# A two-layer attention kernel: transposes of the normalized activations moved from TensorE to a DMA and ScalarE, and one product ordered in four pieces

## The chip, the cores and the metric

The kernel runs on one core of one Trainium2 chip. The metric is the device time of one execution in microseconds (us), as a median of a few runs. The profile is of one execution, taken by the hardware profiler.

## The reference, cut to what matters

The input `x` is 16 sequences of 512 tokens with 128 features, in 32-bit floats. Two layers follow, and each has an attention and a feed-forward part, both behind a normalization without weights and both added to `x`:

```python
def _layernorm(x, axis=-1, eps=1e-05):
    m = jnp.mean(x, axis=axis, keepdims=True)
    v = jnp.var(x, axis=axis, keepdims=True)
    return (x - m) / jnp.sqrt(v + eps)
...
    x = x + _L0_attn_ref(_layernorm(x, axis=-1), ...)
    x = x + _L0_ffn_ref(_layernorm(x, axis=-1), ...)
    x = x + _L1_attn_ref(_layernorm(x, axis=-1), ...)
    x = x + _L1_ffn_ref(_layernorm(x, axis=-1), ...)
```

Each attention has 16 heads of width 8 and a softmax over 512 keys. Layer 1 also normalizes queries and keys. The feed-forward part of layer 0 is a gated one (silu, hidden width 384). That of layer 1 is a linear map plus a mixture of low-rank corrections ("lora"): for each token, 8 experts are weighted by a softmax, and a product of rank 8 per expert is added.

What matters for the change: every one of the four parts needs the normalized activations transposed (features on the 128 partitions, tokens along the row), since TensorE contracts over partitions.

## The kernel before, in words

**Units.** One unit is one attention of one sequence in one layer: 16 sequences by 2 layers make 32 units. The list `units` (line 1238) starts with six units of layer 0 (`LAG`), then takes layer 1 and layer 0 in turn, and ends with six units of layer 1.

**The two big loops.** For each unit, `maxima` (line 827) computes 64 score products of 512 columns on TensorE, two at a time into a pair of PSUM banks (line 849), and VectorE takes the row maxima of each pair (line 862). The maxima are split into three 16-bit parts on GpSimd, transposed by a DMA (line 896) and written into the stacked queries, so that the second score product already has the maximum subtracted. `scores` (line 905) computes these second products (line 919), again two at a time, and ScalarE takes the exponential of each pair (line 933). `values` (line 938) multiplies the exponentials with the values and accumulates in the bank `acc` (line 950). A "step" is one such multiplication with its two pairs of exponentials: 16 steps a unit, 512 in all.

**PSUM.** Eight banks: three pairs that the maxima and the scores share, a single bank `one` that the other products use one after another (a pair stands in when `one` is taken), and `acc`.

**Around a unit.** `pre(n)` (line 695) makes the queries, keys and values of unit n: `layer_norm` (line 508), the transpose, the projections, and for queries and keys a split into 16-bit parts that six DMAs each (line 679) put into the stacks `qst` and `kst`. It begins when the scores reach step 16 (n - 3) + 3, and the maxima of unit n wait for both stacks. In layer 1 the queries and keys go through a normalization on GpSimd and six DMA transposes (line 652) first, so this chain is the longest. `post(n)` (line 993) is what follows the attention: the division, the output projection, the second normalization and the feed-forward part, `ffn0` or `ffn1`.

**The transposes.** `transposed` (line 561) makes four 128x128 transposes on TensorE into one bank (line 566), and ScalarE copies the bank to SBUF as `xT` (line 569). It is called by `pre` and, for layer 1's feed-forward part, by `post`. `halves` (line 541) serves layer 0's feed-forward part: the same four transposes (line 548), then ScalarE copies the bank twice, once rounded as `x1` (line 551) and once whole as `xT` (line 553), and GpSimd takes the difference `x2` (line 557). There are 32 calls from `pre`, 16 of `transposed` from `post` and 16 of `halves`.

**The lora product.** At the end of `ffn1` (lines 1224 to 1230) 8 small products for each sequence (four token blocks, base weights and lora weights) are issued as one block of work on TensorE.

**What sets the order.** Nothing is left to a scheduler on the chip: each engine runs its instructions in the order in which the program issues them, and a class `Plan` sets that order while the program is built. Each piece of work is a generator that yields an engine, an estimated duration, a priority and what it waits for, with a third pair of numbers for DMAs. `Plan.run` (line 181) always takes the piece that could start first by its own estimates; among those that could start within a small margin on one engine, the lowest priority number wins. On TensorE, `choose` (line 156) weighs the five kinds of work: "m" (maxima), "e" (scores), "v" (values), "x" (small products in column tiles) and "w" (full-array work such as the transposes), by constants such as `UM`, `UB`, `LATE`, `AHEAD`. `LEAD`, `LEADE` and `SHRINK` set how many steps the maxima run ahead of the scores, and how that lead shrinks near the end. `MAXPR` is the priority of the maxima's DMAs.

**Idle filler.** Before the first "v" and behind the last, TensorE is given dummy products (line 449).

Of the kernel before, what the change touches and what calls it, by code (L numbers as in the profile page):

```python
# [10 lines left out]
F32 = mybir.dt.float32  # L11
BF16 = mybir.dt.bfloat16
I32 = mybir.dt.int32
F32R = mybir.dt.float32r
AF = mybir.ActivationFunctionType
ALU = mybir.AluOpType
# [5 lines left out]
P = 128  # L22
S = 512
C = 4
# [20 lines left out]


LAG = 6
LEADE, SHRINK = 12, 2
LEAD = 19
NP = 8  # L50
VLAG = 1.59
# [5 lines left out]
HALF = 3561  # L57
GATE1 = 12000.0
EARLY = 2
MAXPR = 9.8  # L60
MAXT = 2400
DENL = 2800
PAIR = 13.08
STACK = (2600, 700)
TRANS = (3000, 500)
AHEAD = 508
DELAY = 450
UM = {"m": 1.03, "e": 1.02, "v": 0.0, "x": -0.23, "w": -0.04}
UB = {"m": 1660, "e": 1199}
LATE = 5.33  # L70
LATE_M = 2
SAME = 0
SAMEC, NEXT = 0.05, 0.0
# [18 lines left out]
def act(n, ptr=0):  # L92
    return 51 + n / 1.2 + 93 * ptr
# [218 lines left out]
def encoder_kernel(ctx: ExitStack, tc: tile.TileContext, x, wf, wi, lb, cols, rows, out):  # L312
    nc = tc.nc
# [15 lines left out]
    banks = Pairs(pairs, [single])  # L329
# [3 lines left out]
    def ring(tag, shape=None, dt=F32, bufs=2):  # L333
        if tag not in rings:
            rings[tag] = Ring(sb, shape, dt, tag, bufs)
        return rings[tag]
# [3 lines left out]
    r_xn, r_xT = ring("xn", [P, C, P]), ring("xT", [P, S])  # L340
    r_x1, r_x2 = ring("x1", [P, S], F32R, 1), ring("x2", [P, S], F32R, 1)
    r_a = [ring(f"a{k}", [P, S], BF16) for k in (1, 2, 3)]
# [8 lines left out]
    r_p = ring("p", [P, 2, S], bufs=NP)  # L351
    r_av, r_num = ring("av", [P, S]), ring("num", [P, S])
    r_y = ring("y", [P, S])
    r_den, r_rdb = ring("den", [P, 64]), ring("rdb", [P, S], bufs=1)
    r_h, r_th, r_ub = ring("h", [P, NF, S], bufs=1), ring("th", [P, S]), ring("ub", [P, S], bufs=1)
    r_lg, r_mid, r_mx = ring("lg", [P, C, E]), ring("mid", [P, C, R]), ring("mx", [P, C])
# [11 lines left out]
    w = const.tile([P, WEND], F32, name="w")  # L368
# [5 lines left out]
    ident = const.tile([P, P], F32, name="ident")  # L374
# [133 lines left out]
    def layer_norm(b_, nm, pr, waits, alone=False):  # L508
# [29 lines left out]
        r_rs.give(krs, t)  # L538
        return xn, kxn, t

    def halves(xn, kxn, t, nm, pr):

        t = yield "PE", 440, pr(), "w", (t, banks.one, r_xT, r_x1)
        b, pt = banks.take1()
        xT, kxT = r_xT.take(f"xT{nm}")
        x1, k1 = r_x1.take(f"x1{nm}")
        for c in range(C):
            nc.tensor.transpose(pt[:, c * P : (c + 1) * P], xn[:, c], ident)
        r_xn.give(kxn, t)
        tx = yield "ACT", act(S), pr(), None, (t,)  # L550
        nc.scalar.activation(x1, pt, AF.Copy)
        t = yield "ACT", act(S), pr(), None, (t,)
        nc.scalar.activation(xT, pt, AF.Copy)
        banks.give(b, t)
        t = yield "POOL", 1180, pr(), None, (t, tx, r_x2)
        x2, k2 = r_x2.take(f"x2{nm}")
        nc.gpsimd.tensor_tensor(x2, xT, x1, ALU.subtract)
        r_xT.give(kxT, t)
        return (x1, k1, tx), (x2, k2, t)

    def transposed(xn, kxn, t, nm, pr):
        t = yield "PE", 440, pr(), "w", (t, banks.one, r_xT)
        b, pt = banks.take1()
        xT, kxT = r_xT.take(f"xT{nm}")
        for c in range(C):
            nc.tensor.transpose(pt[:, c * P : (c + 1) * P], xn[:, c], ident)  # L566
        r_xn.give(kxn, t)
        t = yield "ACT", act(S), pr(), None, (t,)
        nc.scalar.activation(xT, pt, AF.Copy)
        banks.give(b, t)  # L570
        return xT, kxT, t
# [123 lines left out]
    def pre(n):  # L695
        b_, layer = units[n]
        nm = f"a_{b_}_{layer}"
        base = 16 * (n - 3) + PRE0
        pr = ramp(base, base + PRELEN, 34 if layer else 16)
# [3 lines left out]
        if layer == 0 and b_ > 0:  # L703
            t = yield "SP", 500, pr(0), None, (r_xt, gate), (2700, 700)
            load_x(b_)
            at["xt", b_, 0] = t
        xn, kxn, t = yield from layer_norm(b_, nm, pr, (("xt", b_, layer), gate), n < EARLY)
        xt = xt_of[b_]
        xT, kxT, tT = yield from transposed(xn, kxn, t, nm, pr)
        at.setdefault("go", tT)  # L710

        def residual():
# [6 lines left out]
        if layer:  # L719
            kq = None  # L720
            for g in range(2):
                t = yield "PE", 880, pr(), "x", (tT, banks.one, r_qk if g == 0 else 0.0)
                b, pt = banks.take1()
# [9 lines left out]
                t = yield "DVE", dve(S), pr(), None, (t,)  # L733
# [12 lines left out]
                t = yield "DVE", 600, pr(), None, (tg, r_ms if g == 0 else 0.0)  # L746
# [10 lines left out]
            t = yield "DVE", 400, pr(), None, (t, r_ri)  # L757
# [6 lines left out]
            t = yield "POOL", 400, pr(), None, (t, r_rt)  # L764
            nc.gpsimd.tensor_tensor(msf, msf, mhalf, ALU.mult)
            rt, krt = r_rt.take(f"rt{nm}")
            for _ in range(3):
                for k in range(4):
                    t = yield "POOL", 400, pr(0.5), None, (t - 80,)
# [11 lines left out]
            for g in range(2):  # L781
                gs = slice(8 * g, 8 * g + 8)
                t = yield "POOL", 1270, pr(), None, (t - 80,)
# [7 lines left out]
        if layer:  # L791
            t = yield "POOL", 1280, pr(), None, (t - 80, "qkn")
# [3 lines left out]
        for qk in (1, 0):  # L796
# [4 lines left out]
            t = yield "PE", 860, pr(), "x", (tT, "w", banks.one, safe, r_t, r_a[0])  # L801
            b, pt = banks.take1()
# [5 lines left out]
        t = yield "PE", 4 * 224, pr(), "x", (tT, "w", banks.one, ("stack", n), ("fill", n % NST))  # L808
        b, pt = banks.take1()
# [348 lines left out]
    def ffn1(b_, xt, xT, kxT, tT, tr, alone, pr):  # L1158
        nm = f"_{b_}_f1"
        t = yield "PE", 4 * 60, pr(), "x", (tT, banks.one, r_lg, r_mid, r_mx)  # L1160
        bl, pl_ = banks.take1()
        lg, klg = r_lg.take(f"lg{nm}")
        mid, kmid = r_mid.take(f"mid{nm}")
        mx, kmx = r_mx.take(f"mx{nm}")
        pl = pl_[:, : C * 16].rearrange("p (c k) -> p c k", c=C)
        for c in range(C):
            product(pl[:, c], xT[:, c * P : (c + 1) * P], w[:, WRA1 : WRA1 + 16])
        if alone:
            ta = yield "PE", 4 * 224, pr(0), "w", (tT, banks.one)
            bb, pb = banks.take1()  # L1170
            for c in range(C):
                nc.tensor.matmul(
                    pb[:, c * P : (c + 1) * P],
                    xT[:, c * P : (c + 1) * P],
                    w[:, WB1 : WB1 + P],
                    start=True,
                    stop=True,
                )
        t = yield "DVE", 450, pr(), None, (t,)
        nc.vector.tensor_tensor(  # L1180
            lg, pl[:, :, :E], row[:, None, RB1 : RB1 + E].to_broadcast([P, C, E]), ALU.add
        )
        nc.vector.tensor_copy(mid, pl[:, :, E:])
        nc.vector.tensor_reduce(mx, lg, AX.X, ALU.max)
        nc.vector.tensor_tensor(
            lg, lg, mx[:, :, None].to_broadcast([P, C, E]), ALU.subtract
        )
        banks.give(bl, t)
        t = yield "ACT", 100, pr(), None, (t,)
        nc.scalar.activation(lg, lg, AF.Exp)  # L1190
        t = yield "DVE", 200, pr(), None, (t,)
        nc.vector.tensor_reduce(mx, lg, AX.X, ALU.add)
        nc.vector.reciprocal(mx, mx)
        t = yield "POOL", 200, pr(), None, (t, r_gt)
        gt, kgt = r_gt.take(f"gt{nm}")
        nc.gpsimd.tensor_tensor(gt, lg, mx[:, :, None].to_broadcast([P, C, E]), ALU.mult)
        r_lg.give(klg, t)
        r_mx.give(kmx, t)
        t = yield "POOL", 620, pr(), None, (t, r_cf)
        cf, kcf = r_cf.take(f"cf{nm}")  # L1200
        nc.gpsimd.tensor_tensor(
            cf[:, :, :E],
            gt[:, :, :, None].to_broadcast([P, C, E, R]),
            mid[:, :, None, :].to_broadcast([P, C, E, R]),
            ALU.mult,
        )
        r_gt.give(kgt, t)
        r_mid.give(kmid, t)
        if alone:
            ta = yield "DVE", dve(S), pr(), None, (ta, tr)  # L1210
            nc.vector.tensor_tensor(xt, pb.rearrange("p (c d) -> p c d", c=C), xt, ALU.add)
            banks.give(bb, ta)
        t = yield "PE", 440, pr(), "w", (t, banks.one, r_cT)
        b, pc = banks.take1()
        cT, kcT = r_cT.take(f"cT{nm}")
        for c in range(C):
            nc.tensor.transpose(  # L1217
                pc[:, c * P : (c + 1) * P], cf[:, c].rearrange("p e r -> p (e r)"), ident
            )
        r_cf.give(kcf, t)  # L1220
        t = yield "ACT", act(S), pr(), None, (t,)
        nc.scalar.activation(cT, pc, AF.Copy)
        banks.give(b, t)
        t = yield "PE", 8 * 218, pr(), "x", (t, banks.one)
        b, pt = banks.take1()
        for c in range(C):
            cs = slice(c * P, (c + 1) * P)
            if not alone:
                product(pt[:, cs], xT[:, cs], w[:, WB1 : WB1 + P], stop=False)
            product(pt[:, cs], cT[:, cs], b2, start=alone)  # L1230
        r_xT.give(kxT, t)
        r_cT.give(kcT, t)
        t = yield from add_psum(xt, pt, b, (t, tr), pr, alone, nm)
        t = yield "SP", 440, pr(), None, (t,), (2300, 500)
        nc.sync.dma_start(out[b_].rearrange("(c p) d -> p c d", p=P), xt)
        r_xt.give(xtk[b_], t)
# [126 lines left out]
```

## Time and profile before

| what | before |
|---|---|
| median of 3 runs | 1544.62 us (1544.41 to 1546.84) |
| the profiled execution's own time | 1544.07 us |
| its span, first to last instruction | 1542.0 us |
| TensorE busy | 1473.2 us in 14744 instructions |
| VectorE busy | 1412.8 us |
| ScalarE busy | 1270.3 us |
| GpSimd busy | 943.3 us |
| DMA queue fed by SyncE | 131.61 MB, 32.0% of the 16 DMA engines' time |
| granted TensorE clock | 1.0 of full speed |

How to read it: a busy time is the part of the span in which an engine had an instruction running. TensorE's matmuls overlap one another and the end of each is modelled, so a busy TensorE may still have lost time between starts. Names are those of the program: L862 is line 862, PE is TensorE, PEld its weight loads, DVE VectorE, ACT ScalarE, POOL GpSimd, SP SyncE, which issues nearly all DMAs here ("SPq" is its queue). `nm<-pp` is an instruction that reads the tile `pp` and writes `nm`. A group's row ends with its busy time and the mean duration of one, in ns, and then the idle time of the engine ahead of it, with what ended that idle time.

### The profile page before, as it was taken

How to read it: one execution, taken by the hardware profiler on the slowest of the kernel's cores; microseconds unless marked ns; L12 is line 12 of the kernel's file. 1: busy time of each engine (PE TensorE's matmuls, PEld its weight loads, DVE VectorE, ACT ScalarE, POOL GpSimd, SP SyncE). 2: the span in 40 equal slices, each digit the busy share in tenths (PEclk: the TensorE clock that was granted, in tenths of full speed). 3: DMA queues.
4: the chain of work that ended last, by engine and by line, in shares of the span. 5: the costliest groups of instructions: out<-in, count | busy, mean ns of one | idle time of the engine just before them, and what ended most of it. 6: DMA issues, size and time to landing. Idle time of an engine off the chain costs nothing.

```text
span 1542.0 us, 38016 instructions
## 1 busy us (share of the span) xinstructions
PE 1473.2 (96%) x14744; PEld 505.8 (33%) x14751; DVE 1412.8 (92%) x1874; ACT 1270.3 (82%) x1552; POOL 943.3 (61%) x1241
## 2 busy tenths in 40 slices
PE   8889999999999999999999999999999999999998
PEld 3222333333333333333233333333333233333333
DVE  6999999999999999999999999999999999999874
ACT  2688888888878888888988888888888878988894
POOL 2633467575675747758475675747758776787232
PEclk9999999999999999999999999999999999999999
DMA  4332234223343232433324343232432334434211
GB/s 118 94 90 60 62 85 108 64 68 101 83 105 105 67 94 67 126 84 87 99 62 113 84 118 93 66 95 66 125 84 75 100 81 104 111 92 104 81 55 39
DMA packets 185444, 135.42 MB, mean 88 GB/s; under 512 B 90884, under 2 KB 160612, under 8 KB 185264
## 3 DMA queue, kind: packets, MB, share of 16 engines
q1 hardware_dynamic: 184256, 131.61, 32.0%
q8 instruction: 116, 1.90, 0.6%
q10 hardware_dynamic: 1008, 1.38, 0.3%
q14 instruction: 64, 0.52, 0.1%
HBM read 23.43 MB, written 38.53 MB: 40 GB/s over the span
## 4 chain that ended last, share of the span: by engine, by line
PE 56%; DVE 28%; ACT 7%; issue 6%; DMA 1%; POOL 1%; SPq 0%; ACTq 0%; DVEq 0%; POOLq 0%
DVE nm L862 23%; PE acc L950 18%; PE pp L919 11%; PE pp L849 11%; PE one L458 10%; ACT p L933 5%; PE one L1113 1%; PE acc L449 1%; PE one L1126 1%; PE one L566 1%; DVE th_f L1119 1%; DMA kst<-a11a 1%; POOL xt L585 1%; DVE msa L760 1%; PE one L1217 0%
## 5 line engine op out<-in xcount | busy, mean ns | idle before, releaser
L862 DVE TENSOR_REDUCE nm<-pp 128x2 f32<-128x1024 f32 x1024 | 1204.0, 1218 | 80.4 <-PE pp L849 70.7
L933 ACT ACTIVATE p<-pp 128x1024 f32<-128x1024 f32 x1024 | 1022.5, 1028 | 174.3 <-PE pp L919 152.6
L950 PE MATMUL acc<-p,vst 128*32 128x512 f32 x4096 | 547.8, 604 | 0.7
L849 PE MATMUL pp<-kst,qst 64*128 64x512 bf16 x2048 | 388.7, 380 | 31.3 <-ACT p L933 14.3
L919 PE MATMUL pp<-qst,kst 64*128 64x512 bf16 x2048 | 390.2, 382 | 22.8 <-DVE nm L862 12.0
L919 PEld LDWEIGHTS <-kst 64*128 64x128 bf16 x2048 | 131.4, 93 | 421.6 <-issue 393.9
L849 PEld LDWEIGHTS <-qst 64*128 64x128 bf16 x2048 | 141.7, 94 | 312.5 <-issue 277.4
L950 PEld LDWEIGHTS acc<-p,vst 128*32 128x32 f32 x4096 | 83.1, 108 | 141.3 <-issue 132.6
L967 ACT ACTIVATE av<-acc 128x512 f32<-128x512 f32 x128 | 77.5, 605 | 20.3 <-PE acc L950 18.3
L606 POOL TENSOR_TENSOR t1a<-t1a,a11a 128x512 f32<-128x512 f32 x14 | 16.2, 1160 | 116.1 <-ACT a11a L601 116.1
L585 POOL TENSOR_TENSOR xt<-y,xt 128x512 f32<-128x512 f32 x31 | 39.5, 1275 | 77.8 <-ACT y L582 77.8
L1136 POOL TENSOR_TENSOR h_f<-th_f,ub_f 128x512 f32<-128x512 f32 x48 | 61.2, 1275 | 30.4 <-ACT ub_f L1133 30.4
L458 PE MATMUL one<-w,xTa 128*32 128x128 f32 (+1 forms) x1504 | 67.7, 313 | 0.4 <-DVE th_f L1119 0.4
L885 POOL CAST mp<-nm 128x32 bf16<-128x32 f32 x62 | 13.0, 210 | 87.0 <-DVE nm L862 87.0
L590 POOL TENSOR_TENSOR xt<-xt,row 128x512 f32<-128x512 f32 x48 | 61.2, 1276 | 6.6 <-DVE row L479 5.4
L1030 POOL TENSOR_TENSOR num<-num,rdb 128x512 f32<-128x512 f32 x31 | 39.6, 1276 | 30.9 <-DMA rdb<-drd 30.7
L585 POOL TENSOR_TENSOR xt<-y_f,xt 128x512 f32<-128x512 f32 x31 | 39.7, 1280 | 28.4 <-ACT y_f L582 28.1
L458 PE MATMUL one<-wd,h_f 128*32 128x128 f32 x1536 | 55.2, 277 | 0.0
L458 PEld LDWEIGHTS one<-w,xTa 128*32 128x32 f32 x1504 | 38.7, 109 | 25.3 <-issue 14.2
L458 PEld LDWEIGHTS one<-wd,h_f 128*32 128x32 f32 x1536 | 38.0, 109 | 20.0 <-issue 19.5
L784 POOL TENSOR_TENSOR qksa<-qksa,ria 128x512 f32<-128x512 f32 x32 | 40.1, 1274 | 1.3
L449 PE MATMUL acc<-busy 128*128 128x512 bf16 x132 | 34.9, 402 | 2.7 <-DVE busy L398 1.3
(187 smaller groups left out, 1570.1 us busy)
## 6 DMA issues: line engine op xcount, KB each, us to landing
dav<-av SPq DMA_DIRECT2D x127, 256.0 KB
kst<-a11a SPq DMA_DIRECT2D x80, 128.0 KB
qst<-a10a SPq DMA_DIRECT2D x77, 128.0 KB
num<-dav SPq DMA_DIRECT2D x31, 256.0 KB
rdb<-drd SPq DMA_DIRECT2D x31, 256.0 KB
kst<-a21a SPq DMA_DIRECT2D x48, 128.0 KB
kst<-a01a SPq DMA_DIRECT2D x48, 128.0 KB
qst<-a00a SPq DMA_DIRECT2D x48, 128.0 KB
```

The costliest lines, as they stand in the source:

```text
L449: nc.tensor.matmul(acc, busy[:, :P], busy, start=True, stop=True)
L458: nc.tensor.matmul(out[js], lhs[:, js], rhs, start=start, stop=stop, tile_position=(0, 32 * j))
L585: nc.gpsimd.tensor_tensor(xt, y.rearrange("p (c d) -> p c d", c=C), xt, ALU.add)
L590: nc.gpsimd.tensor_tensor(xt, xt, row[:, None, lo : lo + P].to_broadcast([P, C, P]), ALU.add)
L784: nc.gpsimd.tensor_tensor(qkv4[:, gs], qkv4[:, gs], ri[:, gs, None, :].to_broadcast([P, 8, HD, 8]), ALU.mult,)
L849: nc.tensor.matmul(pt[:, k], qst[n % NST][band, t, qc * P : (qc + 1) * P], kst[n % NST][band, t], start=True, stop=True,)
L862: nc.vector.tensor_reduce(nm[:, :, t % T, qc] if half1 != half else nm[:, half, t % T, qc : qc + 2], pt, AX.X, ALU.max, negate=True,)
L919: nc.tensor.matmul(pair[:, half], kst[n % NST][band, t, kc * P : (kc + 1) * P], qst[n % NST][band, t], start=True, stop=True,)
L933: nc.scalar.activation(pt, pair, AF.Exp, scale=SCALE)
L950: nc.tensor.matmul(acc[32 * j : 32 * j + 32], vst[n % NST][:, kc, lo : lo + 32], p_of[n, i, kc, j // 2][0][:, j % 2], start=(kc == 0), sto ...
L967: nc.scalar.activation(av, acc, AF.Copy)
L1136: nc.gpsimd.tensor_tensor(h[:, f], th, ub, ALU.mult)
```

## The change

A new generator `planes` takes the place of the TensorE transposes in `pre` for all units but the first two (30 calls), and in `halves` (16 calls). It has three steps. ScalarE copies the 128x512 activations, seen as 128x1024 numbers of 16 bits, so that the 512 high and the 512 low halves form two planes. One DMA transpose, issued by SyncE, transposes the 128x1024 block. ScalarE copies the 1024 transposed 16-bit numbers back into 32-bit words. In `halves`, `x1` is then copied from `xT` in SBUF and no longer from PSUM. `transposed` stays for the first two units and for layer 1's feed-forward part.

At the end of `ffn1` the product is yielded in four pieces of one token block each (two pieces for the last unit), so that other TensorE work can be ordered between them.

Eight constants of the planner have new values.

```diff
-LEADE, SHRINK = 12, 2
+LEADE, SHRINK = 12, 3
...
-MAXPR = 9.8
+PLANES = 2
+MAXPR = 10.66
...
-AHEAD = 508
+AHEAD = 445
 DELAY = 450
-UM = {"m": 1.03, "e": 1.02, "v": 0.0, "x": -0.23, "w": -0.04}
-UB = {"m": 1660, "e": 1199}
-LATE = 5.33
+UM = {"m": 1.03, "e": 1.02, "v": 0.0, "x": 0.04, "w": 0.26}
+UB = {"m": 1537, "e": 1274}
+LATE = 4.58
...
+    r_u, r_z = ring("u", [P, 2, S], U16), ring("z", [P, 2 * C, P], U16)
...
+    def planes(xn, kxn, t, nm, pr):
+
+        t = yield "ACT", act(2 * S), pr(), None, (t, r_u)
+        u, ku = r_u.take(f"u{nm}")
+        nc.scalar.activation(
+            u, xn.rearrange("p c d -> p (c d)").bitcast(U16).rearrange("p (s k) -> p k s", k=2), AF.Copy
+        )
+        r_xn.give(kxn, t)
+        e = yield "SP", 1300, pr(), None, (t, r_z), (2600, 700)
+        z, kz = r_z.take(f"z{nm}")
+        nc.sync.dma_start_transpose(z, u.rearrange("p k s -> p (k s)"))
+        r_u.give(ku, e)
+        t = yield "ACT", act(2 * S), pr(), None, (e, r_xT)
+        xT, kxT = r_xT.take(f"xT{nm}")
+        nc.scalar.activation(
+            xT.bitcast(U16).rearrange("p (s k) -> p k s", k=2),
+            z.rearrange("p (k c) s -> p k (c s)", k=2),
+            AF.Copy,
+        )
+        r_z.give(kz, t)
+        return xT, kxT, t
+
     def halves(xn, kxn, t, nm, pr):
 
-        t = yield "PE", 440, pr(), "w", (t, banks.one, r_xT, r_x1)
-        b, pt = banks.take1()
-        xT, kxT = r_xT.take(f"xT{nm}")
+        xT, kxT, t = yield from planes(xn, kxn, t, nm, pr)
+        tx = yield "ACT", act(S), pr(), None, (t, r_x1)
         x1, k1 = r_x1.take(f"x1{nm}")
-        for c in range(C):
-            nc.tensor.transpose(pt[:, c * P : (c + 1) * P], xn[:, c], ident)
-        r_xn.give(kxn, t)
-        tx = yield "ACT", act(S), pr(), None, (t,)
-        nc.scalar.activation(x1, pt, AF.Copy)
-        t = yield "ACT", act(S), pr(), None, (t,)
-        nc.scalar.activation(xT, pt, AF.Copy)
-        banks.give(b, t)
-        t = yield "POOL", 1180, pr(), None, (t, tx, r_x2)
+        nc.scalar.activation(x1, xT, AF.Copy)
+        t = yield "POOL", 1180, pr(), None, (tx, r_x2)
...
-        xT, kxT, tT = yield from transposed(xn, kxn, t, nm, pr)
+        how = planes if n >= PLANES else transposed
+        xT, kxT, tT = yield from how(xn, kxn, t, nm, pr)
...
-        t = yield "PE", 8 * 218, pr(), "x", (t, banks.one)
-        b, pt = banks.take1()
+        b, tl = None, t
         for c in range(C):
+            if c % 2 == 0 or not alone:
+                n_ = 4 * 218 if alone else 2 * 218
+                t = yield "PE", n_, pr(0.5), "x", (tl, banks.one if b is None else 0.0)
+            if b is None:
+                b, pt = banks.take1()
```

More of the change, by code (lines that the diff above doesn't have):

```diff
@@ L13 @@
 I32 = mybir.dt.int32
+U16 = mybir.dt.uint16
 F32R = mybir.dt.float32r
```

## The prediction

> **What bounds the kernel now.** I read the page's first part, then the chain of work that ended last.
>
> ```profile
> PE 1473.2 (96%) x14744; PEld 505.8 (33%) x14751; DVE 1412.8 (92%) x1874; ACT 1270.3 (82%) x1552; POOL 943.3 (61%) x1241
> ...
> PE 56%; DVE 28%; ACT 7%; issue 6%; DMA 1%; POOL 1%; SPq 0%; ACTq 0%; DVEq 0%; POOLq 0%
> ```
>
> TensorE carries 56% of the chain, and 62% with the issue time, VectorE 28%, ScalarE 7%. No engine bounds alone. The middle of the run, by stretches, says the same:
>
> ```profile
> 100.00:1450.00 1350.00, 1303.71 (x13224) 445.55 (x13217) 1271.60 (x1664) 1151.53 (x1409) 877.25 (x1140) 1.00 0.34 90
> ```
>
> The busy times are PE, PEld, DVE, ACT and POOL: 97%, 94% for VectorE, 85% for ScalarE, at a full clock. The waits in that stretch (who waited for whom, us in all, times, longest) show how they hang together:
>
> ```profile
> ACT p L933 <- PE pp L919: 127.6, 247, 1.6
> ...
> DVE nm L862 <- PE pp L849: 61.9, 161, 1.5
> ```
>
> Of VectorE's 78 us of idle time (1350 - 1271.6), 62 are waits for TensorE, and ScalarE waits for it too. But TensorE isn't saturated either: after a score pair, the next pair of the other kind starts 0.224 us later in the median, 0.298 in the mean, over 1092 such steps. It waits there for a PSUM pair that VectorE or ScalarE holds: 1092 x 0.074 = 81 us.
>
> **What leaves TensorE.** One transpose in the timeline (start, duration):
>
> ```profile
> 699.91 0.60 PE L566 MATMUL pp<-ident,xnf 128*128 128x128 f32 x4
> ...
> 700.51 0.39 PE L849 MATMUL pp<-kst,qst 64*128 64x512 bf16 x2
> ```
>
> The four transposes hold TensorE from start to next start for 0.6 us. They go by 0.109 us from start to start (median of the trace). From a pair's last start to a transpose are 0.316 us, and from the last transpose's start to a pair 0.206. Without a change of kind these would be 0.224 (pair to pair) and 0.109 (transpose to transpose), so a change between half-array, column-tile and full-array work costs (0.522 - 0.333) / 2 = 0.095. I count in the two instruction orders: transposes on TensorE fall from 256 to 72, so 46 calls go, 46 x 4 x 0.109 = 20.1 us. Changes of kind fall from 1724 to 1670, which includes what the lora pieces add: 54 x 0.095 = 5.1 us. Sum: **25.2 us** of TensorE time. Through the chain's 62% that is 25.2 x 0.62 = **-15.6 us**; with VectorE wholly behind it, all 25.2 could count; with ScalarE late, none.
>
> **What comes to ScalarE.** No row shows a 16-bit copy of 1024 with a stride. The nearest:
>
> ```profile
> L933 ACT ACTIVATE p<-pp 128x1024 f32<-128x1024 f32 x1024 | 1022.5, 1028 | 174.3 <-PE pp L919 152.6 <-DVE nm L862 13.3 <-ACT cT_f L1222 1.3
> ...
> L569 ACT ACTIVATE xTa<-one 128x512 f32<-128x512 f32 x31 | 18.6, 599 | 8.0 <-PE one L566 8.0
> ...
> L629 ACT ACTIVATE b00a<-qksa 128x512 bf16<-128x512 f32 x16 | 10.1, 630 | 0.2
> ...
> L553 ACT ACTIVATE xTf<-one 128x512 f32<-128x512 f32 x16 | 10.0, 622 | 0.0
> ...
> L419 ACT ACTIVATE qst<-zero 128x2048 f32<-128x2048 f32 x1 | 1.9, 1910 | 0.0
> ```
>
> From SBUF, 512 elements take 0.63 and 2048 take 1.91: 0.83 ns an element, so 1.06 for 1024. Bounds: 0.85 (the elements alone) and 1.91 (if a strided 16-bit access ran at half pace, the row of 2048). I take 1.06, as the 16-bit output of L629 goes at the pace of the others. `pre`: 30 x (2 x 1.06 - 0.60) = 45.6; `halves`: 16 x (2 x 1.06 - 0.62) = 24.0, the copy `x1` staying. Sum **70 us** (51 to 148 by the bounds), which lifts ScalarE to some 90% of the middle stretch.
>
> **The new wait.** ScalarE's second copy waits for the DMA, in order, and the exponentials behind it wait too; so then does TensorE, for a pair. Between the two copies the new order holds this much other ScalarE work, at the rows' durations: 2.6 us in 12 cases, 3.0 to 3.2 in 5, 3.6 in 14, over 3.6 in 15. Existing transposes, issue to the last step of the landing: 128x128 (L896) 2.27 us in the median, 128x512 (L652) 2.45 to 3.18 by tile, with nine in ten under 3.2 to 4.3. One row of these in SyncE's queue:
>
> ```profile
> L652 SPq DMA_TRANSPOSE a00a<-b00a x16: 1191/1233/2419, 251.3 to 1411.1; - x16
> ```
>
> Three more blocks of 128 cost 0.4 (2.67 for this tile, against 2.27), so eight blocks land in about 2.67 + 4 x 0.13 = 3.2; ends: 2.4 (the fastest with four blocks) and 4.3. With 0.15 for the hand-overs, 12 x 0.75 + 3 x 0.35 + 2 x 0.15 = **10 us** of ScalarE stalls (0 to some 40). The 80 us count as ScalarE's time does today, 7% of 1542 = 108 of 1270 busy, so 8.5%: **+6.8 us**.
>
> A rule speaks against this. In the Trainium skill, the page "VectorE: DVE Perf Modes", section "Rules for kernel authors", would do a 128x128 transpose on TensorE wherever a result in PSUM will do, and its section "The three transpose paths" puts it at 390 ns there and 1309 ns by the DMA. By an estimate from that page, eight blocks in turn would land in 10.5 us, and the 46 stalls would come to some 320 us. The rows differ: four blocks land only 0.4 us after one, so I keep 3.2.
>
> **Other parts.** *SyncE* issues 46 more transposes: 46 x 1.25 = 58 us on a queue whose instructions take 722 of 1542 us. Behind them in the queue stand the writes of `av` (L973, 383 us of waiting for ScalarE), which have the slack of that waiting, and the DMAs of the maxima (L896, L899), whose results are used steps later; that cover gone, each is 1.25 later. The *DMA engines*, at 34%, get 46 x 1024 packets of 0.020 us over 16 engines, 59 us or 4 points. I cost both at nothing. *GpSimd* and *VectorE* lose no instruction.
>
> The *lora block*: in the middle units its 32 products hold TensorE for 1.71 us, and in that time and 1.5 us behind it VectorE idles 0.43 and ScalarE 1.04. Four pieces end part of that; the extra changes of kind are in the count above. 15 x 0.43 = 6.4, of which I take half: **-3 us** (0 to -6.4).
>
> The *end*: in the old order 12.5 score steps stand behind the last maximum, in the new 11. Such a step takes 2.2 us (1489 to 1516.7), against 2.9 in the middle. If VectorE sets the pace up to there, 1.5 x 2.2 = 3.3 go; if TensorE does, none: **-2 us**.
>
> Sum: -15.6 + 6.8 - 3 - 2 = -13.8. Against the profiled execution's 1544.07 (span 1542.0 and 2.07 around it), 1530.3; the median is 0.55 higher, so **1531**.
>
> **Rivals.**
> 1. *VectorE is freed*: all 25.2 us of TensorE time count, ScalarE's share hides in its 200 us of idle time, and the lora pieces and the end give 5. 1544.6 - 30.2 = 1514. For: 62 of VectorE's idle 78 us are waits for TensorE. Against: that asks VectorE for 96% in the middle.
> 2. *ScalarE takes back what TensorE gives*: as it nears 90%, 26% of the 80 us count in place of 8.5%, 20.6 us against 20.6 gained: 1544.6, no change. Then pairs are held by exponentials. For: TensorE's waits for a pair held by L933 exist already (14.3 us at L849). Against: the exponentials run up to eight deep ahead of the values.
> 3. *The unpacking copy waits for its DMA*, and ends slower. If the eight blocks land in 4.0, the upper tenth of the rows, the covers of 2.6 to 3.8 us fall short by 12 x 1.55 + 3 x 1.15 + 2 x 0.95 + 14 x 0.55 + 0.35 = 32 us, all in front of exponentials. -20.6 + 6 + 32 = +17: 1562. It decides from a landing of about 3.5, where the stalls eat the gain if all lie on the path. For: the DMA shares one queue with the stack writes. Against: many of these exponentials wait for TensorE anyhow (127.6 us).
> 4. *Layer 1's chain comes late*: the last write of its stack is issued 7.2 us ahead of the first maximum (units 8 to 24, median), and such writes land in 2.8, so 4.4 are to spare. The way from activations to `xT` grows from 1.9 to 1.06 + 3.2 + 0.2 + 1.06 = 5.5, by 3.6. With 2 us more of queueing, the 13 units with margins like this (7 to 9) lose 1.2 to 2 each: about +20 against -14, 1551. In layer 0 the margin is 16 us.
>
> That the change doesn't do what it says is out: the orders show the transposes gone.
>
> **Chances.** Forecast 0.46 (1531; own range 1522 to 1540), rival 1 0.16 (1514), rival 2 0.12 (1544.6), rival 3 0.18 (1562), rival 4 0.08 (1551). Faster than 0.2%, about what a measurement can tell here, 0.62; within 0.2% 0.12; slower 0.26. The range runs from 1513 to 1560: it takes in half of rivals 1 and 3 and the others whole, which leaves out under 2 in 10. ScalarE's upper bound of 148 us belongs to what lies above.
>
> **What would show it.** Right: both new copies near 1.06 us; transposes landing in 3.2; TensorE's busy time down by some 25 us with its gaps between pairs no longer than 0.298 in the mean; VectorE over 95% in the middle. Wrong: ScalarE idle ahead of the second copy by over 20 us in all, ended by the DMA; exponentials that TensorE waits for by over 40 us; maxima that start on the landing of a stack write; copies of 1.5 us and more.

## The result, and the profile after

| what | before, beside it | after |
|---|---|---|
| median | 1544.84 us | 1615.04 us (4 runs, 1611.18 to 1620.21) |
| ratio, 95% interval | 1 | 1.0454 (1.0417 to 1.0491) |
| profiled execution, its span | 1544.07, 1542.0 us | 1611.92, 1610.1 us |

The kernel is 70 us slower, far outside the predicted range. The page's first part and its chain of work, after:

```profile
PE 1476.2 (92%) x14558; PEld 480.8 (30%) x14564; DVE 1412.1 (88%) x1874; ACT 1336.2 (83%) x1598; POOL 943.2 (59%) x1241
...
PE 49%; DVE 16%; ACT 14%; issue 8%; DMA 8%; POOL 3%; SPq 1%; ACTq 0%; DVEq 0%; POOLq 0%
```

VectorE's share of the chain falls from 28% to 16%. ScalarE and the DMAs, 8% together before, carry 22%. TensorE's busy time doesn't fall, though some 180 of its matmuls are gone: the windows show why. The same middle stretch as before (busy PE, PEld, DVE, ACT, POOL with their instructions, then granted clock, DMA share, GB/s):

```profile
100.00:1450.00 1350.00, 1243.05 (x12416) 401.99 (x12419) 1205.97 (x1578) 1159.61 (x1389) 839.76 (x1083) 0.98 0.38 94
```

Every engine gets through fewer instructions in these 1350 us (ScalarE is even busy 8 us longer), and the mean clock is 0.98. Who waits for whom, on ScalarE (us in all, times, longest):

```profile
ACT p L951 <- PE pp L937: 139.2, 244, 13.8
ACT xTa L558 <- DMA za<-ua: 38.5, 21, 4.9
```

and on TensorE:

```profile
PE pp L867 <- ACT p L951: 47.9, 43, 5.2
PE pp L937 <- ACT p L951: 24.2, 46, 2.0
```

TensorE's waits for exponentials grow from 18.7 us (14.3 + 4.4 at the same two products) to 72.1, and the longest from 0.7 to 5.2. The groups of ScalarE, with the new ones (instructions, busy time, mean ns, idle time ahead of them and what ended it):

```profile
L951 ACT ACTIVATE p<-pp 128x1024 f32<-128x1024 f32 x1024 | 1014.9, 1028 | 159.3 <-PE pp L937 139.2 <-DVE nm L880 8.7 <-ACT th_f L1135 3.5
...
L558 ACT ACTIVATE xTa<-za 128x1024 uint16<-128x1024 uint16 x30 | 40.9, 1364 | 38.8 <-DMA za<-ua 38.5
L548 ACT ACTIVATE ua<-xna 128x1024 uint16<-128x1024 uint16 x30 | 31.7, 1058 | 4.8 <-POOL xna L539 4.6
...
L558 ACT ACTIVATE xTf<-zf 128x1024 uint16<-128x1024 uint16 x16 | 21.6, 1352 | 1.6 <-DMA zf<-uf 1.6
```

ScalarE idles 38.8 us ahead of `pre`'s second copies, and only 1.6 ahead of those of `halves`.

**Where in the run.** From the first score of one unit to that of the next (worked out from the trace's start times), summed:

| intervals | before | after | difference |
|---|---|---|---|
| first six | 287.6 us | 299.0 us | +11.5 |
| 7th, 9th, ... 23rd (nine) | 428.6 | 488.1 | +59.5 |
| 8th, 10th, ... 24th (nine) | 407.7 | 403.4 | -4.3 |
| last seven | 314.7 | 315.5 | +0.8 |

From the 7th to the 24th, every second interval loses 6.6 us. One of these, in the timelines. ScalarE (start, duration, in brackets the idle time ahead and what ended it):

```profile
767.64 1.06 ACT L548 ACTIVATE ua<-xna 128x1024 uint16<-128x1024 uint16 x1
...
771.53 2.86 ACT L951 ACTIVATE p<-pp 128x1024 f32<-128x1024 f32 x3 [0.94 <-PE pp L937]
778.17 1.34 ACT L558 ACTIVATE xTa<-za 128x1024 uint16<-128x1024 uint16 x1 [3.79 <-DMA za<-ua]
779.38 0.99 ACT L951 ACTIVATE p<-pp 128x1024 f32<-128x1024 f32 x1
```

SyncE's issues in the same time:

```profile
767.14 0.63 SPq L917 DMA_DIRECT2D qst<-msb  x1
767.83 0.63 SPq L685 DMA_DIRECT2D qst<-zero  x1
768.51 1.87 SPq L696 DMA_DIRECT2D qst<-a00a  x3
770.42 1.26 SPq L696 DMA_DIRECT2D qst<-a10a  x2
772.04 0.56 SPq L696 DMA_DIRECT2D qst<-a20a  x1
772.71 1.39 SPq L991 DMA_DIRECT2D dav<-av  x1
774.21 0.40 SPq L1257 DMA_DIRECT2D out_dram<-xt  x1
774.65 1.33 SPq L554 DMA_TRANSPOSE za<-ua  x1
```

TensorE:

```profile
775.94 0.39 PE L937 MATMUL pp<-qst,kst 64*128 64x512 bf16 x2
780.43 1.04 PE L867 MATMUL pp<-kst,qst 64*128 64x512 bf16 x4 [4.09 <-ACT p L951]
```

The first copy ends at 768.70. The transpose is issued at 774.65, 5.95 us later: SyncE has been issuing almost without a break since 756, and the transpose is the last of that run. From issue to the second copy are 3.52. Exponentials stand behind that copy on ScalarE, so no pair comes free, and TensorE stops for 4.09 us. From the middle of that gap on, from 778.76 to 785.59, the clock stands at 0.5 (same columns as the middle stretch above):

```profile
774.00:778.00 4.00, 2.34 (x20) 0.59 (x17) 2.65 (x3) 0.38 (x1) 3.75 (x4) 1.00 0.79 200
778.00:782.00 4.00, 1.21 (x6) 0.38 (x5) 0.86 (x1) 3.83 (x5) 0.00 (x0) 0.60 0.07 26
782.00:786.00 4.00, 4.00 (x20) 0.65 (x22) 2.62 (x3) 2.27 (x3) 0.00 (x0) 0.55 0.44 105
```

From 782 to 786 TensorE counts as wholly busy with 20 matmuls, at a clock of 0.55; eight products of `values` that start at 782.37 take 1.93 us, where eight that start at 774.91, at the full clock, take 1.07. Over the run the clock stands at 0.5 for 65.4 us in twelve stretches of up to 6.8. Nine of them go with TensorE gaps of 3.1 to 5.2 us: they begin 2.0 to 4.7 us after the gap's start, seven of them before its end. Before, there are 2.0 such us, at the end.

So it goes through the kernel: of 30 transposes in `pre`, nine wait 4.3 to 6.0 us from the end of the first copy to the issue (47.6 us over the 30; 0.5 over the 16 of `halves`). These nine are the layer-0 units' transposes, due while SyncE works through a layer-1 unit's six transposes and stack writes.

### The profile page after: what moved, and what is told of

The parts are those of the page before. It is cut to its first block, busy times and chain, and to the rows that moved or that the text cites. A ratio compares the mean times of both kernels' runs of the same rounds, so it can differ in the third digit from the quotient of the medians.

```text
span 1610.1 us, 37606 instructions
## 1 busy us (share of the span) xinstructions
PE 1476.2 (92%) x14558; PEld 480.8 (30%) x14564; DVE 1412.1 (88%) x1874; ACT 1336.2 (83%) x1598; POOL 943.2 (59%) x1241
## 3 DMA queue, kind: packets, MB, share of 16 engines
q10 hardware_dynamic: 1008, 1.38, 0.3%
## 4 chain that ended last, share of the span: by engine, by line
PE 49%; DVE 16%; ACT 14%; issue 8%; DMA 8%; POOL 3%; SPq 1%; ACTq 0%; DVEq 0%; POOLq 0%
PE acc L968 17%; DVE nm L880 14%; PE pp L937 10%; ACT p L951 10%; PE pp L867 9%; PE one L461 8%; DMA za<-ua 5%; PE one L1144 1%; PE acc L452 1%; ACT av L985 1%; PE one L1131 1%; DMA xt<-in_x_dram 1%; ACT ua L548 1%; ACT xTf L558 0%; SPq L696 0%
## 5 line engine op out<-in xcount | busy, mean ns | idle before, releaser
L968 PE MATMUL acc<-p,vst 128*32 128x512 f32 x4096 | 557.2, 613 | 2.4 <-ACT av L985 1.8
L867 PE MATMUL pp<-kst,qst 64*128 64x512 bf16 x2048 | 397.4, 388 | 69.7 <-ACT p L951 47.9
L867 PEld LDWEIGHTS <-qst 64*128 64x128 bf16 x2048 | 132.4, 94 | 416.8 <-issue 392.5
L558 ACT ACTIVATE xTa<-za 128x1024 uint16<-128x1024 uint16 x30 | 40.9, 1364 | 38.8 <-DMA za<-ua 38.5
L1048 POOL TENSOR_TENSOR num<-num,rdb 128x512 f32<-128x512 f32 x31 | 39.5, 1275 | 54.2 <-DMA rdb<-drd 24.1
L574 POOL TENSOR_TENSOR x2f<-xTf,x1f 128x512 fp32r<-128x512 f32 x16 | 20.4, 1274 | 53.5 <-ACT x1f L571 53.5
L525 POOL TENSOR_SCALAR rsa<-mva 128x4 f32<-128x4 f32 x32 | 7.3, 228 | 65.3 <-DVE mva L521 65.3
```

The lines of the kernel that those rows point to most:

```text
L558: nc.scalar.activation(xT.bitcast(U16).rearrange("p (s k) -> p k s", k=2), z.rearrange("p (k c) s -> p k (c s)", k=2), AF.Copy,)
L867: nc.tensor.matmul(pt[:, k], qst[n % NST][band, t, qc * P : (qc + 1) * P], kst[n % NST][band, t], start=True, stop=True,)
L968: nc.tensor.matmul(acc[32 * j : 32 * j + 32], vst[n % NST][:, kc, lo : lo + 32], p_of[n, i, kc, j // 2][0][:, j % 2], start=(kc == 0), sto ...
L1048: nc.gpsimd.tensor_tensor(num, num, rdb, ALU.mult)
```

## The experiments

**Theory:** the 70 us come from the second copy's wait for a DMA stuck in SyncE's queue, with the halved clock behind it. **Rivals:** the copies take ScalarE's time (1.8 us for each transpose come to an engine at 85%); or the new order (the eight constants) costs it, and the planes don't. In the first three experiments every engine runs the instructions that are left in the same order as in the kernel after. Each kernel ran beside the kernel before, whose median was 1544.8 to 1545.5.

**1. The second copy reads a constant.** DMA, copy and order stay; only the wait goes. The transposed activations are left out.

```diff
         nc.scalar.activation(
             xT.bitcast(U16).rearrange("p (s k) -> p k s", k=2),
-            z.rearrange("p (k c) s -> p k (c s)", k=2),
+            zero.bitcast(U16).rearrange("p (k s) -> p k s", k=2),
             AF.Copy,
```

> The changed kernel with every instruction in the same order, but the second ScalarE copy reads a constant tile of zeros instead of the transposed planes, so that it waits for no DMA (the transposed activations are left out, so later numbers are not the reference's). Theory A, that ScalarE's in-order wait for the DMA, which stands late in SyncE's queue, makes the loss: in the changed kernel the 12 layer-0 units of the middle take 54 us instead of 47, and the others 44.5 instead of 45.3; without the wait all go at the lower pace: 1515 to 1535 us. Rival B, that ScalarE's 78 us of added copies are too much beside the exponentials: 1590 to 1615, as the copies stay. Rival C, that the planner's new constants gave a worse order: 1590 to 1615 too.

Measured: 1555.7 us, ratio 1.0067 (1.0050 to 1.0084). Its group of second copies:

```profile
L558 ACT ACTIVATE xTa<-zero 128x1024 uint16<-128x1024 uint16 x30 | 41.2, 1372 | 0.0
```

The copies take as long as before, the idle time is gone, the slow intervals fall from 54.2 to 49.2 us in the mean (47.6 before), and the clock is halved for 17.1 us in place of 65.4. The wait, with the halved clock that goes with it, costs 1615.0 - 1555.7 = **59 us** of the 70. That the kernel would then be faster than the one before (1515 to 1535 us) didn't come true.

**2. The same, with both copies cut to 16 elements a partition**, in constant tiles. The transposed activations are left out here too:

```diff
-            u, xn.rearrange("p c d -> p (c d)").bitcast(U16).rearrange("p (s k) -> p k s", k=2), AF.Copy
+            u[:, :, :8],
+            xn.rearrange("p c d -> p (c d)").bitcast(U16).rearrange("p (s k) -> p k s", k=2)[:, :, :8],
+            AF.Copy,
...
-            xT.bitcast(U16).rearrange("p (s k) -> p k s", k=2),
-            z.rearrange("p (k c) s -> p k (c s)", k=2),
+            xT.bitcast(U16).rearrange("p (s k) -> p k s", k=2)[:, :, :8],
+            zero.bitcast(U16).rearrange("p (k s) -> p k s", k=2)[:, :, :8],
```

> As the run with the constant tile, and both ScalarE copies cut to 16 elements, so that neither the wait nor ScalarE's 110 us of copies are left (the transposed activations are left out; the DMA still transposes a tile of the same size); the order is the same. Theory A2, that the TensorE time which the change sets free is real and ScalarE's copies take it back: 1515 to 1535 us, 20 to 40 under the 1555.7 with the copies. Rival C, that the order made by the new constants holds the rest of the loss: 1545 to 1560.

Measured: 1542.57 us, 0.9982 (0.9967 to 0.9997). Its copies take 0.22 us. 46 x (1.06 + 1.36 - 0.44) = 91 us of ScalarE time cost 1555.7 - 1542.6 = **13 us**. What is left, without wait and copies, is within 3 us of the kernel before: the nine pairs of middle units take 92.2 us each in place of 92.9, and the first eight units lose 10. This lies between the two ranges expected. The time that TensorE gains and what the new order costs aren't told apart here, but together they leave nothing of the 70 us.

**3. The queue: fewer issues ahead of the transposes.** The order stays; the stack writes of layer 1's queries are left out, 96 of SyncE's 988 DMAs (and with them that part of the result).

```diff
-                nc.sync.dma_start(stack[slot], part[which])
+                if qk or units[n][1] == 0 or n < NST:
+                    nc.sync.dma_start(stack[slot], part[which])
```

> The changed kernel in the same order, without the six SyncE writes of the layer-1 units' queries into their stack (90 writes; that part of the computation is left out, old queries stay). These stand in SyncE's queue right ahead of the transposes of the layer-0 units that come late. If SyncE's full queue makes them late: the time from the end of the first copy to the issue of the transpose falls from 4.3 to 6.0 us in 10 units to under 2, ScalarE's idle time ahead of the second copy from 38.7 to under 15 us, the 54 us units to 48 to 50, and the whole to 1545 to 1580 us. If the lateness comes from the landing or from something else: 1600 to 1615.

Measured: 1576.49 us, 1.0207 (1.0186 to 1.0228). The time from first copy to issue falls from 47.6 to 20.8 us in all, and ScalarE's waits:

```profile
ACT xTa L558 <- DMA za<-ua: 12.6, 19, 2.1
```

With the DMA, its size and the order unchanged, fewer writes in front of it take away 26 of these 38.5 us, and 38.5 us of the time (1615.0 - 1576.5). The landing of `pre`'s transposes is 3.21 us in the median, against 3.25 in the kernel after. This shows that the queue made the wait, not the landing. (Whether the lighter load of the DMA engines gained something elsewhere isn't told apart.) The clock is halved for 11.8 us.

**4. Telling the planner.** Three runs, with the changed landing, SyncE's cost of layer 1's transposes as measured, and the planes for layer 1 alone:

```diff
-        e = yield "SP", 1300, pr(), None, (t, r_z), (2600, 700)
+        e = yield "SP", 1300, pr(), None, (t, r_z), (8600, 700)
```

> The changed kernel with the planner's estimate of the transpose's landing raised from 2600 to 8600 ns, so that 7.6 to 14.5 us of other ScalarE work stand between the two copies (2.6 to 8.2 in the changed kernel). Theory A: the copy finds its data landed, 1520 to 1550 us; the upper end if layer 1's chain, 6 us longer, now comes late. Rival B (too much ScalarE work): 1590 to 1615. Rival C (constants): 1590 to 1615.

Measured: 1568.68 us, 1.0155 (1.0140 to 1.0171). The issue comes as late as ever (61.6 us in all), but 8.5 to 15.5 us pass between the copies, filled with other work, and ScalarE never idles ahead of the second one. Of the 59 us, 46 are saved (1615.0 - 1568.7); the time is still 19 us above the range expected.

```diff
-            e = yield "SP", 600, pr(0.2), None, (t, r_a[k]), TRANS
+            e = yield "SP", 1250, pr(0.2), None, (t, r_a[k]), TRANS
```

> The changed kernel with the planner's cost of layer 1's six transposes on SyncE raised from 600 to 1250 ns, which is what the trace shows; the planner then knows that SyncE's queue is full when a layer-0 unit's planes are ready, and puts 7 to 10 us of work between the copies in many of these units. Theory A with SyncE's queue as the reason of the delay: 1520 to 1560 us. If the delay comes from the DMA itself and not from the queue: above 1590. Rivals B and C: 1590 to 1615.

Measured: 1596.39 us, 1.0330 (1.0304 to 1.0357). The waits fall only to 26.5 us, and the time to issue, in all, is 52.8 us, not less than the 47.6: the planner's wrong price for SyncE is not what makes the transposes late. The time is in the range that was set for a DMA that is slow by itself, but the landing is 3.18 us in the median, as ever.

```diff
-        how = planes if n >= PLANES else transposed
+        how = planes if layer else transposed
```

> The changed kernel with planes in layer 1's attention and layer 0's feed-forward part only; layer 0's attention, whose transposes stood behind SyncE's burst, goes back to TensorE. The order is planned anew. Theory A: ScalarE's idle time ahead of the second copies falls from 40 to under 12 us, and the time to 1550 to 1595, the rest being the order, since the same constants without any planes gave 1610. If the stalls come anyway, in other places: 1600 or more.

Measured: 1592.57 us, 1.0290 (1.0259 to 1.0321). The waits for `z` are down to 7.2 us, as the theory has it, but the order is another, and brings a wait of its own:

```profile
PE pp L937 <- DMA qst<-msb: 20.4, 9, 3.7
```

**5. The parts by themselves.** The kernel after with TensorE transposes (new constants, lora pieces); the kernel after with the eight old constants; the kernel before with the lora pieces alone; the kernel before with the eight new constants alone.

```diff
-PLANES = 2
+PLANES = 99
...
-        xT, kxT, t = yield from planes(xn, kxn, t, nm, pr)
+        t = yield "PE", 440, pr(), "w", (t, banks.one, r_xT, r_x1)
...
```

> The changed kernel without the planes: TensorE transposes everywhere again, the new constants and the lora pieces kept. Theory A: no wait, no loss, 1535 to 1560 us. Rival C (the constants and the pieces make the loss): 1590 or more. Rival B: 1535 to 1560, as theory A.

```diff
-LEADE, SHRINK = 12, 3
+LEADE, SHRINK = 12, 2
...
-UB = {"m": 1537, "e": 1274}
-LATE = 4.58
+UB = {"m": 1660, "e": 1199}
+LATE = 5.33
```

> The changed kernel with all eight constants of the planner at their old values; planes and lora pieces kept. Between the copies of layer-0 units then stand 3.2 to 6.8 us of other work in the middle, by the order. Theory A (the wait is the loss): the wait shrinks with longer cover but SyncE's queue is as full, 1570 to 1610 us. Rival C (constants): 1535 to 1560.

```diff
-        t = yield "PE", 8 * 218, pr(), "x", (t, banks.one)
-        b, pt = banks.take1()
+        b, tl = None, t
         for c in range(C):
+            if c % 2 == 0 or not alone:
...
```

> The kernel before with the lora product in four pieces and nothing else. If the pieces are harmless: 1538 to 1550 us. If they make the loss that is left when the planes are taken out of the changed kernel (1610): 1590 or more.

```diff
-LEADE, SHRINK = 12, 2
+LEADE, SHRINK = 12, 3
...
-UB = {"m": 1660, "e": 1199}
-LATE = 5.33
+UB = {"m": 1537, "e": 1274}
+LATE = 4.58
```

> The kernel before with the eight new constants and nothing else. Rival C (the constants make the loss of the kernel without planes): 1590 to 1620 us. If the lora pieces make it: 1535 to 1560.

| kernel | median us | ratio (95%) |
|---|---|---|
| after, TensorE transposes | 1610.43 | 1.0428 (1.0392 to 1.0464) |
| after, old constants | 1639.56 | 1.0606 (1.0585 to 1.0626) |
| before, lora pieces | 1545.11 | 0.9996 (0.9986 to 1.0005) |
| before, new constants | 1599.76 | 1.0346 (1.0329 to 1.0363) |

The lora pieces alone do nothing. The new constants without planes cost 54.5 us, the planes without the new constants 94.3, and both together 70: the parts don't add up, since each set of constants makes another order. TensorE's waits in the kernel before with the new constants:

```profile
PE pp L919 <- DMA qst<-msb: 16.3, 7, 3.1
...
PE one L458 <- POOL num L1030: 11.2, 8, 3.1
```

By the ranges set beforehand, the first and the last row speak for the constants. But these kernels run other orders than the kernel after, and their waits are others: in the kernel after TensorE waits 0.9 us for `msb` and not at all for `num`. Its own order costs nothing once the wait and the copies are gone (experiment 2), so the 54.5 can't be counted into its 70. The planes with the old constants were expected at 1570 to 1610 us, and are slower; they have the theory's wait, larger still, and a halved clock for 85.3 us:

```profile
ACT xTa L558 <- DMA za<-ua: 50.5, 15, 5.7
```

**6. The order made anew.** The planner gets the measured costs (below), and its weights are searched again, by its own estimate of the end: with all planes, with planes for layer 1 and `halves` (two results of the search), with none (two results), and for `halves` only.

```diff
-LEADE, SHRINK = 12, 3
-LEAD = 19
+LEADE, SHRINK = 12, 7
+LEAD = 20
...
-VLAG = 1.59
+VLAG = 1.58
...
-MAXPR = 10.66
+MAXPR = 10.65
...
-AHEAD = 445
+AHEAD = 316
...
-UB = {"m": 1537, "e": 1274}
-LATE = 4.58
+UB = {"m": 1565, "e": 1271}
+LATE = 6.22
...
-POST0 = 3.31
-POSTLEN = 20
+POST0 = 3.29
+POSTLEN = 20.10
...
-        t = yield "ACT", act(2 * S), pr(), None, (t, r_u)
+        t = yield "ACT", 1060, pr(), None, (t, r_u)
...
-        e = yield "SP", 1300, pr(), None, (t, r_z), (2600, 700)
+        e = yield "SP", 1300, pr(), None, (t, r_z), (4000, 700)
...
-        t = yield "ACT", act(2 * S), pr(), None, (e, r_xT)
+        t = yield "ACT", 1360, pr(), None, (e, r_xT)
...
-            e = yield "SP", 600, pr(0.2), None, (t, r_a[k]), TRANS
+            e = yield "SP", 1250, pr(0.2), None, (t, r_a[k]), TRANS
...
-        how = planes if n >= PLANES else transposed
+        how = planes if layer else transposed
```

That is the whole edit of the second kernel of the table; the others differ from it in the weights and in where the planes are used.

> The changed kernel with the planner's costs set to what the trace shows (layer 1's transposes 1250 ns on SyncE, the copies 1060 and 1360 ns, the landing of the planes 4000 ns), and its weights searched again for the earliest end by its own account. In the layer-0 units of the middle 12.4 us of other ScalarE work then stand between the copies. Theory A (the wait behind SyncE's queue, for want of a cost in the planner): ScalarE's idle time ahead of the second copies under 8 us, and 1530 to 1555 us. If planes are bad whatever the order: 1565 or more.

> As the run before it, with planes only in layer 1's attention and layer 0's feed-forward part (layer 0's attention transposed by TensorE), and weights searched for that. Theory A: ScalarE's idle time ahead of the second copies under 5 us, 1530 to 1555 us. If planes are bad whatever the order: 1560 or more.

> No planes at all (TensorE transposes everywhere, lora pieces kept), the planner's cost of layer 1's transposes on SyncE at 1250 ns, and its weights searched again in the same way. If the 22 us that the run before gained under the kernel before come from the planes: 1540 us or more. If they come from the new search of the order: 1510 to 1530.

> As the run before it, with the result of another search that ended 6 us later by the planner's own account; it tells how far orders of nearly the same account differ on the chip. If the search makes the gain: 1515 to 1545 us. If the planes do: 1540 or more.

> Planes in layer 0's feed-forward part only (16 of the 46 calls), costs as measured, weights searched for that. No transpose stands behind SyncE's burst, so ScalarE's idle time ahead of the second copies stays under 5 us; if planes pay where they don't wait: 1520 to 1540 us, and if only the search pays, the same as the runs without planes.

> As the run at 1523 us, planes in layer 1's attention and layer 0's feed-forward part, with the result of another search, which by the planner's own account ends 5 us later than that one. If planes that don't wait pay beyond the search: 1520 to 1537 us, under both searched orders without planes (1538 and 1549). If the one at 1523 was a lucky order: 1538 to 1555.

| planes | median us | ratio (95%) |
|---|---|---|
| all | 1559.73 | 1.0084 (1.0056 to 1.0112) |
| layer 1 and `halves` | **1523.45** | 0.9856 (0.9841 to 0.9870) |
| none | 1538.01 | 0.9946 (0.9931 to 0.9961) |
| none, second result | 1548.94 | 1.0021 (1.0012 to 1.0031) |
| `halves` only | 1541.17 | 0.9973 (0.9962 to 0.9985) |
| layer 1 and `halves`, second result | 1562.52 | 1.0113 (1.0096 to 1.0130) |

The kernel at 1523.45 is the best of all. Its middle stretch:

```profile
100.00:1450.00 1350.00, 1307.69 (x13282) 432.36 (x13279) 1279.38 (x1684) 1214.68 (x1463) 879.91 (x1142) 1.00 0.38 97
```

VectorE is at 95% with 1684 instructions, before at 94% with 1664, and the clock is full. In `pre`, 4.3 to 5.4 us pass from issue to the second copy, which finds its data there:

```profile
L558 ACT ACTIVATE xTa<-za 128x1024 uint16<-128x1024 uint16 x16 | 21.9, 1366 | 0.0
L558 ACT ACTIVATE xTf<-zf 128x1024 uint16<-128x1024 uint16 x16 | 21.8, 1361 | 0.3 <-DMA zf<-uf 0.3
```

So a version with planes can be faster than before. That the planes make it so isn't shown: two searched orders with the same planes differ by 39 us (1562.5 and 1523.5), and one without any reaches 1538.0. In the slower of the two, the second copies' waits are only 6.1 us; TensorE waits 16.6 us for `num` of GpSimd there, and 1.5 in the faster one. The ranges set beforehand settle nothing either: 1559.7 and 1538.0 fall between them, 1523.5 and 1562.5 outside all of them, 1548.9 is where planes were to make the gain, and 1541.2 lies with the kernels without planes. What stays open is what the planes are worth under the best order of each kind. Issuing the new transposes from another engine's queue wasn't tried.

## Why the prediction was wrong

**The step that failed: the new wait, and with it "I cost both at nothing" for SyncE.** The prediction counted the cover from the end of the first copy, and set it against the landing, 3.2 us, as if the transpose were issued at once. The landing was right: 3.25 us in the median of `pre`'s, 3.08 for `halves`. But nine transposes were issued 4.3 to 6.0 us late. In place of 10 us of stalls there were 40.4 (38.8 in `pre` and 1.6 in `halves`), and they counted in full and more: 59 us, not 10 x 8.5%.

*What the profile of before showed of it.* The prediction took SyncE's share, 722 of 1542 us, as room. In the trace of before its DMAs come in runs without a break: between 500 and 1300 us, twelve runs of 9.5 to 25 us with 11 to 29 DMAs each and no break over 0.25 us. The end of one that began at 713.4:

```profile
735.35 1.25 SPq L679 DMA_DIRECT2D qst<-a10a  x2
736.65 0.60 SPq L679 DMA_DIRECT2D qst<-a20a  x1
737.35 0.53 SPq L973 DMA_DIRECT2D dav<-av  x1
737.99 0.40 SPq L1235 DMA_DIRECT2D out_dram<-xt  x1
```

The late transpose shown above stands behind the same four pieces of work. The prediction looked at what stands behind the new transposes in that queue, and not at what stands ahead of them.

*Why 40 us of stalls cost 59.* This is an account from the traces, not an experiment: no run parts the stalls from the clock. The kernel of experiment 1 has the same order and no stall. Its waits of TensorE for exponentials:

```profile
PE pp L937 <- ACT p L951: 15.8, 44, 0.8
PE pp L867 <- ACT p L951: 13.7, 40, 1.0
```

Against these 29.5 us, the 72.1 of the kernel after are 42.6 more. TensorE is at work in 46.4 of the 65.4 us of halved clock, and in 13.3 of the 17.1 without the wait (the rest lies in its gaps and at the end of the run). These are 33.1 us more, in which it does about half its work: 16.5 us lost. 42.6 + 16.5 = 59.1. The prediction had no term for the clock, as the clock of before was 1.0.

*When the clock falls.* In the kernel after, each of the nine gaps of 3.1 us and more goes with a clock of 0.5. The Trainium skill, page "TensorE: Matmul & The Clock Gate", section "Why this matters for your kernels", warns of idle gaps of TensorE over about 3 us. The trace agrees for these nine, but the length of a gap isn't the whole rule: the clock also fell after gaps of 1.8 us (at 1302) and 2.4 (at 1008, in the kernel of experiment 1), and not after gaps of 2.0 and 2.3 (at 914 and 1051). The twelve stretches begin whole multiples of 3.413 us apart. Cut into periods of that length, the trace shows TensorE busy for 15 to 47% of each period at whose end the clock fell from full (eleven; the twelfth is the end of the run), and for at least 56% of every period at whose end it stayed. In the kernel of experiment 1 these are 31 to 53% and 56%; in the planes with the old constants the two overlap (up to 58%, from 50%).

**ScalarE, +70 us of work.** The first copy takes 1.06 as predicted, the second 1.36 and not 1.06. By the rows, 30 x (1.06 + 1.36 - 0.60) + 16 x (1.06 + 1.35 - 0.62) = 83 us come to it. Their price was mis-sized: 13 of 91 us in experiment 2, 14% where the prediction took 8.5%.

**TensorE, -15.6 us.** That is 0.49 for each of 32 units. Without wait and copies, the middle units gain 0.35 each ((92.9 - 92.2) / 2), but that kernel also has the other constants; its first eight units lose 10 us, and the whole is only 2.3 us faster. No run shows the term by itself.

**The lora pieces, -3**, are worth 0 (1545.11 against 1545.24 beside it). **The end, -2**: the last seven intervals took 0.8 us longer. Neither matters.

**The rule that spoke against the change.** Eight blocks landed in 3.25 us in the median. The row was right against the estimate of 10.5 us from the Trainium skill, page "VectorE: DVE Perf Modes", section "The three transpose paths".

**The rivals.** Rival 3 named the place, the second copy waiting ahead of exponentials, and even the reason, one queue shared with the stack writes, but priced a landing of 4.0 us and gave 1562. Rival 2's mechanism is there with 13 us. Rival 1 fell: VectorE does less in the middle stretch, not more (1206 against 1272 us). Rival 4 isn't seen: of DMAs TensorE waits only for the maxima's, 0.9 us in all, and for no stack write. Of the signs named for a wrong prediction, two came: idle time of over 20 us ahead of the second copy, and exponentials that TensorE waits for by over 40.

The loss in parts: 59.3 us for the wait (with its share of the clock), 13.1 for the copies, and -2.3 (1542.57 against 1544.84) for all the rest, TensorE, order, lora pieces and end. These are differences from one kernel to the next, so they add up to the 70 by the way they are made, and confirm nothing beyond it.

## What to carry to other kernels

Where a compute engine is made to wait for a DMA in its own order, count from the moment the data is ready to the DMA's landing, with the issuing queue's longest unbroken run ahead of it, and not its mean share: a queue half idle here delayed nine of 30 transposes by 4 to 6 us. A stall in front of the instructions that feed TensorE was paid in full here, and again in halved clock where it left TensorE busy for less than about half of a 3.4 us period. Where the order is planned by hand, a changed part and the constants that go with it can't be priced apart, and an order found by search must be measured: two orders found for the same planes stood 39 us apart.

## What the runs showed of the hardware that was not expected

- ScalarE copies 1024 numbers of 16 bits with a strided input in 1.06 us, and with a strided output in 1.36 (for 32-bit numbers in order, the prediction's estimate from 0.83 ns an element is 1.06).
- A DMA transpose of 128x1024 numbers of 16 bits lands 3.08 to 3.25 us after its issue in the median (4.9 at most), hardly later than one of 128x512 (2.45 to 3.18), and holds SyncE's queue for 1.25 to 1.31 us, as long as a 128x512 one (1.19 to 1.30) and twice as long as a stack write (0.6).
- The halved clock came in stretches of 3.41 or 6.83 us (the one at the end of the run apart), on a grid of 3.413 us, after periods in which TensorE was busy for less than about half.
